# The causal mask of the score maxima: one full-array product per bank, or four products on the diagonal 32x32 parts of the array

## The chip, the cores and the metric

The kernel runs on one core of a Trainium2 chip. The metric is device time in microseconds (us) of one execution, given as the median of several runs. Engines are named as in the profile: PE is TensorE's matmul side, PEld its weight loads, DVE is VectorE, ACT is ScalarE, POOL is GpSimd, SP issues DMAs.

## The reference, cut to what matters

Sixteen sequences of 256 tokens and 128 features pass through two layers. Layer 0 has causal softmax attention with 16 heads of 8 features and a mixture of 8 experts; layer 1 has a retention block and a second mixture of experts. The change lies in layer 0's attention alone:

```python
qvk = (h @ Wqvk).reshape(b, s, 3, H, HD)
q, v, k = (qvk[:, :, 0], qvk[:, :, 1], qvk[:, :, 2])
scores = jnp.einsum('bshi,bthi->bsth', q, k)
mask = jnp.where(jnp.arange(s)[None, :] > jnp.arange(s)[:, None], -jnp.inf, 0.0)
scores = scores + mask[None, :, :, None]
weights = jax.nn.softmax(scores / math.sqrt(d), axis=2)
```

A softmax that is safe against overflow needs the largest allowed score of every row (the maximum over the keys up to the query's own position). Finding these maxima is what `top` does.

## The kernel before, in words

**Operands.** For each sequence `n`, `products` and `keys_and_queries` (L406 to L424) make `kU` and `qM`, float32 tiles of 128 partitions. Head group `j` (0 to 3) owns the 32 partitions `32*j` to `32*j+31`, so a score product of one head contracts over 32 rows: the operands are slices `[r, ...]` with `r = slice(32*j, 32*j+32)`. Such a product uses 32 of the array's 128 rows and all 128 of its columns; the profile writes it 32*128. Four products of different `j` can sit in the array beside each other. A float32 product is two instruction pairs in the trace (a weight load and a matmul each); a bfloat16 product is one pair.

**Maxima.** `top(ops, u, js, nm)` (L439) works on two head groups `js`. It takes a PSUM bank of 128 x 512 per group, first puts the causal mask into it, and then lists the score products that are added on top. The mask is made by a matmul with an identity: `ident_bf` (128x128 bfloat16) is the stationary operand, `cmask` (0 below the diagonal, -1e30 above it, four copies of 128 columns) the moving one. In `u == 0` (queries 0 to 127 against keys 0 to 127) the mask covers all 512 columns of the bank (L448); in `u` = 1 and 2 (queries 128 to 255 against all keys) it covers the second half of each of two 256-column parts (L456), 256 columns in all. `after` then reduces each bank with a DVE maximum into `nm`. Once per sequence `top_rows` transposes `nm` (tile `pm`), copies it (`mT`) and sends it by four DMAs into spare rows of `qM`, so that the weights' products subtract the maxima.

**Weights.** `weights` (L485) makes the transposed scores of the sequence before in two more banks per call, ACT takes the exponential into `pt`, and POOL zeroes what lies above the diagonal. `values` (L538) multiplies with the values (tile `av`, 128 rows by 32 columns of the array, written 128*32) and `project_out` (tile `po`) ends the attention.

**Order.** Each engine's instructions keep the order in which the Python program issues them. In the loop over `n` (L1504) six steps follow each other, three `u` by two pairs of head groups. Each step is one call of `together(top(...), weights(...))`: the two mask matmuls go out while `top` builds its list, and `together` then interleaves the products of the two lists by head group. After each step `fill()` issues a portion of other work: norms and router of layer 0, its gathered experts, the layer 1 retention of blocks that are ready. Some of that work uses the whole array (`pT`, `pxs`, `ptk`, `pret<-q,st`, `plog`), some uses 32-row parts (`psc`, `pw`). All PSUM tiles share eight banks in turn.

**After.** The masks are gone after the last sequence's maxima, at about 363 us. What follows is mostly the layer 1 experts (`ph`, `py`).

Of the kernel before, what the change touches and what calls it, by code (L numbers as in the profile page):

```python
# [21 lines left out]
P = 128  # L22
# [20 lines left out]
def two_layer_kernel(  # L43
# [26 lines left out]
    B, S, D = h.shape  # L70
# [19 lines left out]
    for t0, t1 in ((0, 2), (2, 4), (4, 8)) + tuple((t, t + 4) for t in range(8, NT, 4)):  # L90
# [7 lines left out]
    ident_bf = const.tile([P, P], BF16)  # L98
# [6 lines left out]
        out=before, in_=ones, compare_op=ALU.is_gt, fill=0.0, base=0, pattern=[[1, P]], channel_multiplier=-1  # L105
    )

    cmask = const.tile([P, 4, P], BF16)
    nc.vector.memset(cmask, 0.0)
    nc.gpsimd.affine_select(  # L110
        out=cmask, in_=cmask, compare_op=ALU.is_ge, fill=NEG, base=0, pattern=[[0, 4], [-1, P]], channel_multiplier=1
# [8 lines left out]
    for m, cmp in ((lower, ALU.is_gt), (lower_eq, ALU.is_ge)):  # L120
        nc.vector.memset(m, 1.0)
        nc.gpsimd.affine_select(
            out=m, in_=m, compare_op=cmp, fill=0.0, base=0, pattern=[[1, E], [-1, E]], channel_multiplier=0
# [36 lines left out]
    def bank(shape, name="sc"):  # L160
        return ps.tile(shape, F32, tag="sc", name=name)
# [40 lines left out]
    def matmul(*args, **kw):  # L202
        return pe.matmul(*args, **kw)
# [222 lines left out]
    def project_v(n):  # L426
# [9 lines left out]
        va4 = vas[n % 3].rearrange("p k h (d a) -> p (k h) d a", a=4)  # L436
        dve.tensor_copy(va4[:, :, :, 0:2], pv.rearrange("p k (h a d) -> p (k h) d a", a=2, d=8))

    def top(ops, u, js, nm):  # L439


        kU, qM, _ = ops
        banks = {j: bank([P, 512], "top") for j in js}
        todo = {j: [] for j in js}
        for j in js:
            r = slice(32 * j, 32 * j + 32)
            if u == 0:
                matmul(banks[j], lhsT=ident_bf, rhs=cmask.rearrange("p j k -> p (j k)"), start=True, stop=True)  # L448
                out = banks[j].rearrange("p (s a k) -> p s a k", s=2, a=2)
                for s in range(2):  # L450
                    for a in range(2):
                        todo[j].append((out[:, s, a], qM[r, s, a, 0:P], kU[r, s, 0:P], False, P))
            else:
                s = u - 1
                out = banks[j].rearrange("p (a k) -> p a k", a=2)
                matmul(out[:, :, P:S], lhsT=ident_bf, rhs=cmask[:, 0:2, :], start=True, stop=True)  # L456
                for a in range(2):
                    todo[j].append((out[:, a], qM[r, s, a, P:S], kU[r, s, :], False, S))

        def after():  # L460
            for j in js:
                if u == 0:
                    o = nm[:, 0].rearrange("p (h j) -> p h j", j=4)[:, :, j]
                    i = banks[j].rearrange("p (a k) -> p a k", k=P)
                else:
                    o = nm[:, 1].rearrange("p (h j) -> p h j", j=4)[:, 2 * u - 2 : 2 * u, j]
                    i = banks[j].rearrange("p (a k) -> p a k", a=2)
                dve.tensor_reduce(o, i, AX.X, ALU.max, negate=True)

        return todo, after  # L470
# [1020 lines left out]
    for u in range(3):  # L1491
        together(top(ops[0], u, (0, 1), maxima[0]), top(ops[0], u, (2, 3), maxima[0]))
        if u < 2:
            transpose0(u, 2 - 2 * u, 4)
# [9 lines left out]
    for n in range(B):  # L1504
# [8 lines left out]
        for u in range(3):  # L1513
            for js, others in (((0, 1), (2, 3)), ((2, 3), (0, 1))):
                parts = [weights(ops[n], u, others, pts)]
                if n + 1 < B:
                    parts.insert(0, top(ops[n + 1], u, js, maxima[n + 1]))
                together(*parts)
                next(sums, None)
                fill()  # L1520
                if n + 1 == B:
                    turn(2.0)
# [135 lines left out]
```

## Time and profile before

| | |
|---|---|
| three runs | 753.98, 760.08, 762.68 us (median 760.08) |
| profiled execution | 753.3 us, of which its span is 751.4 us |
| granted TensorE clock, mean | 0.993 |
| PE busy | 713.7 us (95%) in 5621 matmuls |
| PEld busy | 474.0 us (63%) in 5624 weight loads |
| DVE, ACT, POOL busy | 400.0, 358.6, 284.1 us |
| mask matmuls, `top<-cmask,ident_bf` | 44.4 us busy, 189 records; first at 13.6 us, last at 362.8 us |
| score products for the maxima, `top<-kU,qM` | 110.2 us busy, 1024 records |

How to read it: "busy" counts a matmul from its start to a modelled end that includes the way through the array, so busy times of matmuls in a row overlap and a busy PE is not one at its peak. The distance between the starts of two instructions says more. "x2" in a line of the timeline means that two instructions of one kind were merged; "idle before <-releaser" gives the idle time ahead of the instruction on its engine and what ended it. "issue" means that nothing in the profile explains the wait.

### The profile page before, as it was taken

To read this page: it belongs to the slowest core of one execution; us is meant where nothing else is said; L and a number is where in the kernel's file an instruction comes from. 1 tells how busy PE (TensorE), PEld (TensorE's weight loads), DVE (VectorE), ACT (ScalarE), POOL (GpSimd) and SP (SyncE) were. 2 spreads that over 40 slices of the span, in tenths; PEclk is the share of its full clock that TensorE was granted. 3 is DMA by queue.
4 is the path that set the end of the run, shared out by engine and by line. 5 is a ranking of instruction groups with operands and counts; after the bars stand their busy time and mean duration, and the time that the engine had idled before them with its cause. 6 is when DMAs were issued, how large, how long until landed. Compare 5 with 4: busy or idle time off the path is not lost.

```text
span 751.4 us, 14840 instructions
## 1 busy us (share of the span) xinstructions
PE 713.7 (95%) x5621; PEld 474.0 (63%) x5624; DVE 400.0 (53%) x1074; ACT 358.6 (48%) x707; POOL 284.1 (38%) x516
## 2 busy tenths in 40 slices
PE   5999988999999999999999989999999999999997
PEld 3556655766555566556466655666766776767675
DVE  8774876766657566676552556853223223224222
ACT  3477534555576566867665544223232222332222
POOL 3153354787556557676463413345000000121000
PEclk9999999999999999999999999999999999999999
DMA  4114464223333636404222121231000000323011
GB/s 123 23 51 132 126 174 134 36 48 41 56 62 90 147 89 155 99 14 78 60 55 54 24 60 46 69 91 34 1 28 2 1 1 1 43 32 40 31 41 43
DMA packets 79312, 45.73 MB, mean 61 GB/s; under 512 B 17112, under 2 KB 74656, under 8 KB 79232
## 3 DMA queue, kind: packets, MB, share of 16 engines
q1 hardware_dynamic: 62432, 34.84, 16.4%
q0 software_dynamic: 16800, 9.83, 9.9%
q8 instruction: 50, 0.82, 0.4%
q14 instruction: 30, 0.25, 0.1%
HBM read 24.97 MB, written 17.31 MB: 56 GB/s over the span
## 4 chain that ended last, share of the span: by engine, by line
PE 70%; DVE 13%; DMA 5%; POOL 4%; ACT 3%; issue 3%; SPq 1%; DVEq 0%; ACTq 0%; POOLq 0%
PE py L175 20%; PE ph L175 18%; PE top L175 6%; PE av L175 5%; DVE nm L175 4%; DMA x<-ytab 4%; PE wts L175 4%; PE po L175 3%; PE pq L175 2%; PE pret L175 2%; PE pk L175 2%; POOL nz L175 1%; POOL pt L175 1%; ACT xn L175 1%; SPq L175 1%
## 5 line engine op out<-in xcount | busy, mean ns | idle before, releaser
L175 ACT ACTIVATE hT<-ph,b1T 128x512 f32<-128x512 f32 (+1 forms) x134 | 90.1, 678 | 170.0 <-PE ph L175 155.5
L175 PEld LDWEIGHTS py<-fW_sb,hT 128*128 128x128 f32 x1328 | 155.3, 192 | 21.4 <-issue 19.8
L175 PE MATMUL py<-fW_sb,hT 128*128 128x128 f32 x1328 | 157.9, 276 | 0.0
L175 PE MATMUL ph<-xnT,fW_sb 128*128 128x512 f32 x320 | 147.5, 601 | 0.4 <-DVE st L175 0.4
L175 DVE TENSOR_REDUCE nm<-top 128x2 f32<-128x512 f32 (+1 forms) x192 | 122.2, 682 | 35.1 <-PE wts L175 20.5
L175 ACT ACTIVATE pt<-wts 128x512 f32<-128x512 f32 x192 | 104.9, 599 | 63.8 <-PE wts L175 45.7
L175 PE MATMUL wts<-qM,kU 32*128 32x512 f32 (+1 forms) x512 | 120.0, 526 | 1.1 <-DVE come L175 0.5
L175 POOL TENSOR_SCALAR_AFFINE_SELECT pt<-pt 128x512 f32<-128x512 f32 (+1 forms) x96 | 82.6, 882 | 96.4 <-ACT pt L175 89.4
L175 PE MATMUL top<-kU,qM 32*128 32x256 f32 (+1 forms) x1024 | 110.2, 347 | 0.5 <-issue 0.4
L175 PEld LDWEIGHTS ph<-xnT,fW_sb 128*128 128x128 f32 x320 | 58.0, 192 | 62.3 <-issue 57.3
L175 PEld LDWEIGHTS top<-kU,qM 32*128 32x128 f32 x1024 | 72.6, 187 | 30.1 <-issue 26.5
L175 DVE SCALAR_TENSOR_TENSOR x<-py,gate,x 128x128 f32<-128x128 f32 x160 | 48.6, 346 | 70.5 <-PE py L175 70.5
L175 DVE TENSOR_SCALAR hT<-ph,b1T 128x512 f32<-128x512 f32 (+1 forms) x38 | 26.6, 708 | 97.3 <-ACT hT L175 58.4
L175 POOL DMA_DIRECT2D x<-acc x8 | 10.4, 1368 | 158.0 <-issue 115.3
L175 PEld LDWEIGHTS wts<-qM,kU 32*128 32x128 f32 x512 | 47.4, 186 | 8.5 <-DVE nm L175 2.4
L175 POOL TENSOR_SCALAR_AFFINE_SELECT s<-s 128x1024 f32<-128x1024 f32 x32 | 34.9, 1112 | 36.7 <-ACT s L175 36.7
L175 PE MATMUL av<-pt,va 128*32 128x256 f32 (+1 forms) x512 | 45.4, 489 | 2.3 <-POOL pt L175 1.9
L175 PE MATMUL top<-cmask,ident_bf 128*128 128x256 bf16 (+1 forms) x189 | 44.4, 312 | 0.7 <-DVE nm L175 0.5
L175 ACT COPY s<-psc 128x512 f32<-128x512 f32 x64 | 32.7, 603 | 4.7 <-PE psc L175 4.7
L175 PEld LDWEIGHTS av<-pt,va 128*32 128x32 f32 x512 | 14.6, 109 | 28.0 <-issue 19.6
L175 ACT COPY sv<-av 128x512 f32<-128x512 f32 x32 | 18.5, 590 | 24.6 <-PE av L175 10.6
L175 PE MATMUL pq<-xnT,wqk 128*128 128x256 f32 (+1 forms) x80 | 27.4, 458 | 1.2 <-ACT xnT L175 1.1
(242 smaller groups left out, 934.6 us busy)
## 6 DMA issues: line engine op xcount, KB each, us to landing
ytab<-zeros SPq DMA_DIRECT2D x16, 256.0 KB
x<-ytab POOLq DMA_DIRECT2D x16, 256.0 KB, 4.4
fW_sb<-in_L_ffn_W_dram SPq DMA_DIRECT2D x16, 256.0 KB
xtab<-xnw SPq DMA_DIRECT2D x8, 272.0 KB
num<-sv SPq DMA_DIRECT2D x64, 32.0 KB
den<-di SPq DMA_DIRECT2D x16, 128.0 KB
xtab<-xn SPq DMA_DIRECT2D x8, 256.0 KB
acc<-zeros SPq DMA_DIRECT2D x8, 256.0 KB
```

What stands on the lines that cost most here:

```text
L175: ins = f(*args, **kw)
```

## The change

Each mask product is split into four. Part `k` takes rows and columns `32*k` to `32*k+31` of the identity as the stationary operand and the same 32 rows of `cmask` as the moving one, and writes partitions `32*k` to `32*k+31` of the bank. Since the off-diagonal blocks of an identity are zero, the four products together fill the bank as the one did. `tile_position` puts part `k` on the 32x32 part of the array at row `32*k`, column `32*k`.

```diff
+    def mask(o):
+        for k in range(4):
+            r = slice(32 * k, 32 * k + 32)
+            matmul(
+                o[r],
+                lhsT=ident_bf[r, r],
+                rhs=cmask[r, 0 : o.shape[1], :],
+                start=True,
+                stop=True,
+                tile_position=(32 * k, 32 * k),
+            )
 ...
             if u == 0:
-                matmul(banks[j], lhsT=ident_bf, rhs=cmask.rearrange("p j k -> p (j k)"), start=True, stop=True)
+                mask(banks[j].rearrange("p (k n) -> p k n", k=4))
 ...
-                matmul(out[:, :, P:S], lhsT=ident_bf, rhs=cmask[:, 0:2, :], start=True, stop=True)
+                mask(out[:, :, P:S])
```

In the built program PE's list grows from 192 to 768 mask matmuls with a weight load each. Every other instruction stands where it stood, on all engines, and the waits attached to the instructions are as many as before and of the same kinds.

## Prediction

> **What bounds the kernel now.** I read the page first (busy shares and the largest groups), then the table by stretches, PE's waits, and at last the timeline around single masks, PE and its weight loads together.
>
> ```profile
> span 751.4 us, 14840 instructions
> ...
> PE 713.7 (95%) x5621; PEld 474.0 (63%) x5624; DVE 400.0 (53%) x1074; ACT 358.6 (48%) x707; POOL 284.1 (38%) x516
> ...
> L175 PE MATMUL top<-kU,qM 32*128 32x256 f32 (+1 forms) x1024 | 110.2, 347 | 0.5 <-issue 0.4
> ...
> L175 PE MATMUL top<-cmask,ident_bf 128*128 128x256 bf16 (+1 forms) x189 | 44.4, 312 | 0.7 <-DVE nm L175 0.5
> ```
>
> PE is busy nearly all the time, and the masks wait for almost nothing (0.7 us idle in all ahead of them). From the table by stretches and PE's waits up to 366 us, where the masks lie:
>
> ```profile
> 20.00:366.00 346.00, 331.32 (x3248) 207.97 (x3243) 233.26 (x588) 215.38 (x447) 204.09 (x380) 0.99 0.37 85
> ```
>
> ```profile
> PE pT L175 <- DVE wqk L175: 8.0, 1, 8.0
> PE pm L175 <- DVE nm L175: 3.2, 5, 0.9
> PE pxs L175 <- DMA xk<-xtab,idx: 2.4, 2, 1.6
> PE av L175 <- POOL pt L175: 1.9, 2, 1.7
> ```
>
> The columns are the stretch, its length, then busy us and instructions of PE, PEld, DVE, ACT and POOL: PE works 331.3 of 346 us, DVE 233.3. Its waits for others, after the start-up one of 8.0 us, are a few us in all. So time added to PE ahead of 366 us moves the end almost one for one. Now one step of the loop in the timeline (columns: start, length, engine, operation):
>
> ```profile
> 203.19 0.39 PE L175 MATMUL top<-kU,qM 32*128 32x128 f32 x4
> ...
> 203.51 0.11 PEld L175 LDWEIGHTS <-ident_bf 128*128 128x128 bf16 x2
> 203.51 0.61 PE L175 MATMUL top<-cmask,ident_bf 128*128 128x512 bf16 x2
> ...
> 204.05 0.19 PEld L175 LDWEIGHTS top<-kU,qM 32*128 32x128 f32 x2 [0.42 <-issue]
> 204.05 0.38 PE L175 MATMUL top<-kU,qM 32*128 32x128 f32 x2
> ```
>
> The last two of the products at 203.19 start at 203.30 (a narrower window shows them). On one part of the array these follow each other every 0.11 us, so they are through at 203.41; yet the mask's weight load starts only at 203.51. The second mask starts at 203.74 (narrower window). Full 512-column masks in a row start 0.216 us apart, so it is through at 203.95, and the next load waits until 204.05. So each time the array passes from 32*128 to 128*128 or back, some 0.09 to 0.10 us are lost, and the next weights cannot be loaded ahead. I counted every such passage: from 32*128 to mask the median is 0.093 us between the end of the stream and the load's start, from mask to 32*128 it is 0.094. Now a mask after work on the full array:
>
> ```profile
> 201.35 0.71 PE L175 MATMUL po<-wo_sb,wv 128*128 128x128 f32 x4
> ...
> 201.79 0.21 PEld L175 LDWEIGHTS <-ident_bf 128*128 128x128 bf16 x2
> 201.90 0.59 PE L175 MATMUL top<-cmask,ident_bf 128*128 128x512 bf16 x2
> ```
>
> Here the identity is loaded at 201.79, under the last `po` product, and the mask follows without a gap (median 0.003 us over these passages). The kind of array part is the same, so nothing is lost. The last view is a passage that changes the columns alone, full array to 128*32:
>
> ```profile
> 216.63 0.50 PE L175 MATMUL pv<-wqvk_sb,xnT 128*128 128x128 f32 x3
> ```
>
> ```profile
> 217.06 0.16 PEld L175 LDWEIGHTS av<-pt,va 128*32 128x32 f32 x8
> 217.06 2.79 PE L175 MATMUL av<-pt,va 128*32 128x512 f32 x32
> ```
>
> **The change part by part.** The stream itself: a mask of N columns still sends N columns, now through four parts. How parts run together is shown by the two kinds that the kernel has. Products of four row parts overlap (in the step above two `top` and two `wts` start within 0.02 us), and so do four column parts writing one bank: eight `av` loads take 0.16 us, one takes 0.11, so they start 0.007 us apart. I therefore take four mask parts to start 0.007 us apart and run together, 0.216 us for 512 columns and 0.11 for 256. The second bank's part 0 follows the first bank's part 0, loaded ahead as the second four `av` weights are. The group of two masks then ends 3 x 0.007 = 0.02 us later than now. Built in order, the program has 93 such groups: 93 x 0.02 = **+1.9 us**.
>
> The passages: a group's end (mask to 32*128 products) costs 0.094 now, and I keep that. A group's start depends on what stands before it in PE's list. Of the 93, 46 follow work on parts of the array (26 `top`, 8 `psc`, 6 `pw`, 4 `pvar`, one `av`, one `pb`) and lose 0.09 already. The other 47 follow full-array work (`pT`, `po`, `pxs`, `pret<-q,st`, `ptk`, `plog` and others) and lose nothing. With 32*32 masks all 93 change the kind of part. The new loss at 47 is 0.095 us, as from `pv` to `av` above: three `pv` 0.11 apart from 216.63, the last stream over at 216.96, the `av` load at 217.06. On top, the first weights are loaded in the open: `av`'s first matmuls take 0.617 against 0.592 for later ones, 0.025 for 32 float32 columns, so about 0.013 for bfloat16, an estimate by half. 47 x (0.095 + 0.013) = **+5.1 us**. The full identity's load shows 0.011 in the open where the array was switched before, so nothing changes at the 46.
>
> The 576 further pairs need no time of their own: the trace has stretches of 64 PE instructions in 1.0 us, while the densest step (`u` = 0, 48 instructions of products and 16 of masks) will have 64 in about 1.6. No semaphore is added. The -1e30 arrives in the same bank ahead of the same products, so DVE, ACT, POOL and the queues only see PE later.
>
> Sum on PE: +7.0 us. Some of it is taken up where PE waits now: `pm` for `nm` (3.2 us in five places, after DVE reduced eight banks without a pause), `av`, `pxs`. A group adds up to 0.13 us and a sequence about 0.44, so the five `pm` waits alone could take 2.2 if DVE were not itself fed by the later products. I take 1.5, bounds 0 and 3. That leaves **+5.5 us**. The profiled execution, 753.3 us (span 751.4 and 1.9 around it), becomes 758.8. The three runs have a median of 760.1, 6.8 above the profiled one; I carry the difference over: **765.6 us**, +0.7%.
>
> What the trace does not show is a 32*32 product. Bounds: from below, a passage between 32*128 and 32*32 costs nothing since the rows are cut alike; from above, the four parts run one after another. The row nearest to the first is full array to 128*32, rows cut alike, and it loses 0.095; the rows nearest to the second are `av` (four parts, one bank) and `top` (four row parts, four banks), and both overlap. So I take neither bound for the forecast.
>
> A rule speaks against the overlap. The Trainium skill, TensorEngine Tiling (Array Packing), Restrictions and Gotchas, Gotcha 1, says that different row tiles cannot access the same PSUM bank at the same time; the four mask parts lie in different row parts and write one bank. No run here has such a case: `top` and `wts` give each row part its own bank. By that rule the sum would be the serial one of the next paragraphs, by the rows of `av` it is the one above. PSUM — Partial Sum Buffer, Terms (quadrant), in turn says that different 32-partition quadrants of one bank may be accessed at once, which is this case, and I side with that.
>
> **Rivals.** *Serial parts (slower).* If four parts that write one bank exclude each other, a 512-column mask takes 4 x 0.216 in place of 0.216, +0.65, and a 256-column one +0.32. With 64 and 128 of them that is 41 + 41 = 82 us, and with the 5.1 about 87: 847 us. For it: nothing in the trace joins row parts in one bank. Against: `av` writes four quadrants of one bank at full speed. It decides early: from 765.6 to the 1% line (767.7) only 2.1 us are missing, 0.023 us in each of 93 groups, which is a start distance of 0.015 in place of 0.007.
>
> *Free passages (faster).* If 32*32 and 32*128 need no switch, each group's end saves 0.094, and the 0.102 by which the first product's weights are loaded in the open (matmul 0.372 against 0.270): 93 x 0.196 = 18.2 us. The 41 starts after 32*128 work save 0.10 each, 4.2. Less the 7.0, PE gains 15.4: 744.7 us. DVE's reductions (2 x 0.68 = 1.36 us a step against PE's 1.39 in `u` = 1 and 2) would become the bound in part and keep up to half: 745 to 752. Against it: every passage in the trace that changes rows or columns loses 0.09 to 0.10, and only `pm` (128*16, 16 columns used of a full-array part) passes free.
>
> *Full landing.* If the waits take up nothing and the first loads cost 0.025, PE adds 7.6 us, +1.0%: 767.7, on the line.
>
> **How the numbers follow.** About 1% is what a measurement of this kernel can tell from no change: its three runs lie 1.1% apart. The forecast with its full-landing edge has 0.80, serial parts or a part of that 0.12, free passages 0.08. The forecast's own range is 757 to 773: +2 to +8 us on PE, and the median's own scatter. Of its 0.80, 0.50 lies within 1%, 0.28 above, 0.02 below. Faster 0.10, same 0.50, slower 0.40. The range of 755 to 776 leaves out the far ends of both rivals.
>
> **What would show it.** In the profile after: 768 mask matmuls, of 32*32; four starting within 0.03 us; 0.09 between the stream before and the first load at all groups, also after `po` and `pT`; two 512-column masks to the next products 0.55 us after a full-array product (0.52 now), two 256-column ones about 0.34 (0.32 now); PE's share unchanged; `pm`'s waits a little shorter. Mask parts 0.1 us or more apart would make it wrong upwards, products whose weights are loaded under the masks would make it wrong downwards.

## The result, and the profile after

The change makes the kernel slower by half a per cent. Its median is 759.68 us (756.15 to 765.59, 20 runs) against 757.26 us for the kernel before (751.12 to 762.68, 20 runs); the ratio is 1.0048 with a 95% interval of 1.0027 to 1.0069, or +3.6 us (2.0 to 5.2). Ratios and intervals, here and below, are those on record, worked out from all runs and not from the two medians (whose quotient is 1.0032 here). The profiled execution took 759.34 us, of which 757.4 are its span: 6.0 us more than the span before.

From the page of the kernel after: the span, the engines, the queue that brings instructions (columns: packets, MB, share), and the two groups of `top` on PE.

```profile
span 757.4 us, 15995 instructions
...
PE 718.9 (95%) x6200; PEld 475.9 (63%) x6200; DVE 400.5 (53%) x1074; ACT 358.4 (47%) x707; POOL 282.8 (37%) x516
...
q8 instruction: 54, 0.88, 0.5%
...
L175 PE MATMUL top<-kU,qM 32*128 32x256 f32 (+1 forms) x1024 | 109.2, 346 | 0.0
...
L175 PE MATMUL top<-cmask,ident_bf 32*32 32x256 bf16 (+1 forms) x768 | 46.4, 312 | 0.5 <-DVE nm L175 0.4
```

The masks are 768 products of 32*32, and together they are busy for 46.4 us, where 192 full ones (189 recorded) were for 44.4. So the parts run together; one after another they would have shown some 80 us more. Four packets more came through q8 (50 before), and these turn out to matter. The table by stretches and PE's waits up to 366 us, in the columns of the prediction:

```profile
20.00:366.00 346.00, 330.08 (x3740) 206.07 (x3740) 229.46 (x576) 211.20 (x437) 199.12 (x369) 0.99 0.37 85
```

```profile
PE pxs L175 <- DMA xk<-xtab,idx: 3.4, 2, 2.9
PE pm L175 <- DVE nm L175: 3.3, 6, 0.9
PE av L175 <- POOL pt L175: 2.4, 2, 2.1
```

PE's waits did not shrink: `pm` waits 3.3 us (3.2 before), and the wait of `pxs` for the first gathered tokens rose from 2.4 to 3.4. Now a mask behind full-array work in the timeline (start, length, engine, operation):

```profile
188.35 0.61 PE L175 MATMUL po<-wo_sb,wv 128*128 128x128 f32 x4
188.89 0.12 PEld L175 LDWEIGHTS <-ident_bf 32*32 32x32 bf16 x8
188.89 0.61 PE L175 MATMUL top<-cmask,ident_bf 32*32 32x512 bf16 x8
189.43 0.19 PEld L175 LDWEIGHTS top<-kU,qM 32*128 32x128 f32 x2 [0.42 <-ACT ys L175]
189.43 0.38 PE L175 MATMUL top<-kU,qM 32*128 32x128 f32 x2
```

And the next step, a mask behind products on parts:

```profile
190.20 0.39 PE L175 MATMUL top<-kU,qM 32*128 32x128 f32 x4
190.52 0.12 PEld L175 LDWEIGHTS <-ident_bf 32*32 32x32 bf16 x8
190.52 0.61 PE L175 MATMUL top<-cmask,ident_bf 32*32 32x512 bf16 x8
191.06 0.19 PEld L175 LDWEIGHTS top<-kU,qM 32*128 32x128 f32 x2 [0.42 <-issue]
```

In both cases the identity is loaded only when the array is empty (load and mask start together), and the products follow 0.54 us after the first mask. Before, the identity behind `po` was loaded under the last `po` product. Over all recorded groups, the medians from the end of the stream before to the first product after the masks are:

| what stands before the mask | mask columns | before, us | after, us | difference |
|---|---|---|---|---|
| full-array work | 256 | 0.315 | 0.423 | +0.108 |
| full-array work | 512 | 0.530 | 0.638 | +0.108 |
| work on parts | 256 | 0.417 | 0.420 | +0.003 |
| work on parts | 512 | 0.631 | 0.633 | +0.002 |

So PE's list has grown by 47 x 0.108 + 46 x 0.003 = 5.2 us. How little of it arrives is seen where the clock was full in both profiles. The trace is cut at the start of each sequence's `values` (the start of its second copy `sv<-av`):

| stretch of before, us | new passages (x 0.108) | longer after by, us |
|---|---|---|
| 45.6 to 65.0 | 3 (0.32) | -0.26 |
| 65.0 to 83.8 | 4 (0.43) | +0.64 |
| 83.8 to 104.6 | 2 (0.22) | -0.33 |
| 127.0 to 156.5 | 3 (0.32) | +0.13 |
| 156.5 to 184.0 | 5 (0.54) | +0.33 |
| 220.0 to 244.8 | 3 (0.32) | -0.08 |
| 296.6 to 368.2 | 10 (1.08) | +0.09 |
| sum | 30 (3.24) | +0.52 |

A sixth of the local cost arrives. The one stretch that stands out is 104.6 to 127.0 us, with a single new passage and +3.14 us. Something happened there that is not a passage; the experiments went after it. Not all of it need be one thing: the kernel after runs 3.41 us of this stretch at half the granted clock (from 122.5 us), the kernel before none of it.

One thing about all the numbers below: in every profile the granted clock falls to half for 3.4 us (sometimes 6.8, once 10.2) at several places that differ between profiles, and a run's mean clock explains most of the scatter between runs of one kernel (correlation -0.78; 0.01 of mean clock goes with 5.2 us). That is why each comparison needs a dozen runs, and why two spans are not compared by their difference alone.

### The profile page after: what moved, and what is told of

It reads as the page before. It is cut to its first block, busy times and chain, and to the rows that moved or that the text cites. A ratio compares the mean times of both kernels' runs of the same rounds, so it can differ in the third digit from the quotient of the medians.

```text
span 757.4 us, 15995 instructions
## 1 busy us (share of the span) xinstructions
PE 718.9 (95%) x6200; PEld 475.9 (63%) x6200; DVE 400.5 (53%) x1074; ACT 358.4 (47%) x707; POOL 282.8 (37%) x516
## 4 chain that ended last, share of the span: by engine, by line
PE 72%; DVE 11%; DMA 5%; POOL 5%; issue 2%; ACT 2%; SPq 2%; DVEq 0%; ACTq 0%; POOLq 0%
PE py L175 20%; PE ph L175 18%; PE top L175 7%; PE av L175 5%; PE wts L175 4%; DVE nm L175 4%; PE po L175 3%; PE pq L175 3%; DMA x<-ytab 2%; PE pk L175 2%; SPq L175 2%; PE pret L175 2%; DMA den<-di 1%; PE psc L175 1%; POOL nz L175 1%
## 5 line engine op out<-in xcount | busy, mean ns | idle before, releaser
L175 PEld LDWEIGHTS py<-fW_sb,hT 128*128 128x128 f32 x1328 | 157.5, 194 | 21.5 <-issue 20.1
L175 PE MATMUL py<-fW_sb,hT 128*128 128x128 f32 x1328 | 160.3, 278 | 0.0
L175 PE MATMUL ph<-xnT,fW_sb 128*128 128x512 f32 x320 | 145.8, 595 | 0.4 <-DVE st L175 0.4
L175 PE MATMUL wts<-qM,kU 32*128 32x512 f32 (+1 forms) x512 | 117.9, 525 | 0.5 <-DVE nm L175 0.3
L175 PE MATMUL top<-cmask,ident_bf 32*32 32x256 bf16 (+1 forms) x768 | 46.4, 312 | 0.5 <-DVE nm L175 0.4
```

What stands on the lines that cost most here:

```text
L175: ins = f(*args, **kw)
```

## The experiments

Where an expectation speaks of passages, it means the prediction's reason: every change of array part at a mask costs what was read from the trace. Theory C, in some of them: the kernel before had a lucky alignment that any shift spoils. Theory D: the instruction packets fall differently and one of them meets the writes ahead of the first gather.

### The change taken in halves, a probe, and the change again

The helper was made to note whether the product issued last used the full array (`kind["last"]`). The first kernel uses the four parts only behind work on parts, where no passage is added; the second only behind full-array work.

```diff
+        parts = kind["last"] == "part"      # first kernel; the second has == "full"
 ...
-                matmul(banks[j], lhsT=ident_bf, rhs=cmask.rearrange("p j k -> p (j k)"), start=True, stop=True)
+                mask(banks[j].rearrange("p (k n) -> p k n", k=4), parts)
```

> The four diagonal parts are used only for the 46 mask groups whose predecessor in PE's list is work on parts of the array; the 47 that follow full-array work keep the one full product. Theory (the change of the kind of array part ahead of a mask costs, 0.108 us each time, and only where it is new): none of the 46 is new, so within 0.3 us of before, ratio 1.000. Rival (four loads and matmuls in place of one cost by themselves, wherever they stand): 46 of 93 groups, half of the change's +3.6 us, +1.8 us, ratio 1.0024. In the trace the theory wants 0.42 us from the end of the work before to the first product at 256-column groups after part work, as before.

> The other half: diagonal parts only at the 47 groups that follow full-array work, full products at the 46 others. Theory: all of the cost of the change is here, 47 x 0.108 = 5.1 us on PE, +3.6 us in time, ratio 1.005. Rival (cost of the parts themselves): +1.8 us, ratio 1.0024.

Measured (ratio to the kernel before, in brackets its 95% interval): 1.0031 [0.9999, 1.0064] for the half without new passages (760.46 against 757.4 us) and 1.0022 [0.9991, 1.0054] for the half with all of them (759.29). The first should have been 1.000: its groups take the 0.003 us of the table, and no more, in its own trace. So there seems to be a loss that no passage makes, though the interval just reaches 1.000, and the two halves cannot be told from each other.

The third keeps full-array masks and puts one small 32x32 product ahead of each of the 47, so that the array goes to a part and back.

```diff
+        if kind["last"] == "full" and not kind.get("mask"):
+            matmul(
+                banks[js[0]][0:32, 0:64],
+                lhsT=ident_bf[0:32, 0:32],
+                rhs=cmask[0:32, 0, 0:64],
+                start=True,
+                stop=True,
+                tile_position=(0, 0),
+            )
```

> The kernel before, with one small product (32 rows, 32 columns of the array, 64 moving columns, bfloat16, overwritten by the mask at once) ahead of each of the 47 full masks that follow full-array work. Theory: two changes of kind per group, 0.095 + 0.013 + 0.027 stream + 0.09 + 0.011 = 0.236 us in place of 0.003, 47 x 0.233 = 11.0 us on PE. If a fixed share of seven tenths lands (3.6 of 5.2), +7.7 us, ratio 1.010; if waits take up a fixed 1.5 us and the rest lands, +9.5 us, 1.0125. Rival (cost by number of instructions): 47 pairs in place of the change's 576, +0.3 us, ratio 1.000.

Measured: 1.0048 [1.0018, 1.0078]. On PE each probe takes 0.233 us in the trace, 47 x 0.233 = 11 us; 3.6 us arrive. A miss, and the same lesson as the stretches above: here PE time arrives at about a third.

The change itself once more, on the chip of these three:

> The changed kernel once more beside the others, as the yardstick on this chip: +3.6 us, ratio 1.0048, between 1.0027 and 1.0069.

It gave 1.0033 [1.0002, 1.0064].

### Is it any shift at all?

The kernel before again; then the kernel before with its `po` products doubled in the first two sequences (0.9 us on PE), and in all sixteen (6.9 us).

```diff
-        for c in range(2):
-            matmul(po[:, c, :], lhsT=wv[:, c * P : c * P + P], rhs=wo_sb, start=True, stop=True)
+        for _ in range(2 if n < 2 else 1):      # the larger one: range(2)
+            for c in range(2):
+                matmul(po[:, c, :], lhsT=wv[:, c * P : c * P + P], rhs=wo_sb, start=True, stop=True)
```

> The kernel before, unchanged, as a control: ratio 1.000. If its interval leaves out 1.000, or its mean lies 2 us off, the +2 to +3 us of the first three experiments say nothing. Its profile is a second look at the stretches 127 to 156 us and 245 to 297 us, where the first look at the kernel before had other half-clock windows than the rest.

> The kernel before with the two products of the attention's output projection issued twice for the first two sequences only: four full-array product pairs more per sequence, 2 x 0.43 = 0.9 us on PE before 85 us, no new kind of part, no new wait. Theory A (time added to PE lands in part): at most +0.9 us, ratio 1.001 or less. Theory C (the kernel before is in a lucky alignment that any small shift spoils, which would explain that both halves of the change cost 2.5 us each and the whole of it no more): +2.5 us, ratio 1.003.

> The same doubling for all 16 sequences: 16 x 0.43 = 6.9 us of plain full-array products on PE, 15 of them ahead of the last mask. Theory A with the share that the change showed (clock by clock +2.9 of 5.1 us): +3 to +4 us, ratio 1.005. If all of it lands: +6.9, 1.009. Theory C: +2.5 us plus a little.

Measured: 1.0007 [0.9981, 1.0034], 1.0006 [0.9978, 1.0034] and 1.0056 [1.0033, 1.0079]. A shift of 0.9 us costs nothing that can be seen, which speaks against theory C (its 1.003 lies at the edge of the interval). Of the 6.9 us of the large one 4.2 arrive: hardly any at full clock in the stretches from 13 to 105 us, nearly all of the 0.43 per sequence after 127 us.

### The same number of instructions without a passage

Each mask as four full-array products of a quarter of the columns: 768 products, full identity, no new passage. (In its trace a group of masks takes 0.016 us longer than before, 1.4 us over the 93 groups.)

```diff
+            c = slice(k, k + 1) if n == 4 else slice(k // 2, k // 2 + 1)
+            h = slice(0, P) if n == 4 else slice(64 * (k % 2), 64 * (k % 2) + 64)
+            matmul(o[:, c, h], lhsT=ident_bf, rhs=cmask[:, c, h], start=(k == 0), stop=True, ...)
```

> Each mask as four full-array products of a quarter of its columns: as many mask matmuls and loads as the change (768), the same columns in all, no new kind of part. Theory A (the new passages cost): the loads stay hidden for 128 columns (0.053 us of stream against about 0.011 for the identity), for 64 columns (0.027) just so, within 0.5 us, ratio 1.000. Theory B (the number of instructions costs): as the change, ratio 1.003 to 1.005. Theory C: +2.5 us.

Measured: 1.0025 [1.0002, 1.0048]. Most undisturbed stretches are longer by 0.05 us or less (0.10 at most where the clock is full, but for one of 0.58), yet the stretch from 104.6 to 127 us by 3.42. What stands out without passages sits in this one place (which again holds 3.41 us of half clock). What lies there is the first gather of tokens for the experts (`xk<-xtab,idx`, POOL), which reads a table that SP's queue has just written (`xtab<-xnw`, two writes). SP and POOL in the timeline, first of before, then of after:

```profile
112.05 0.72 SPq L175 DMA_DIRECT2D xtab<-xnw  x1
112.87 0.80 SPq L175 DMA_DIRECT2D dc<-dd  x1
...
116.76 1.25 POOL L175 DMA_INDIRECT xk<-xtab,idx  x1 [3.15 <-DMA ytab<-zeros]
```

```profile
112.36 0.85 SPq L175 DMA_DIRECT2D xtab<-xnw  x1
113.31 0.98 SPq L175 DMA_DIRECT2D dc<-dd  x1
...
118.61 1.25 POOL L175 DMA_INDIRECT xk<-xtab,idx  x1 [4.29 <-DVE dr L175]
```

SP issues the last write 0.31 us later, but the gather leaves 1.85 us later: 6.25 us behind the write in place of 4.71. SP's own issues of these two DMAs take 0.13 and 0.18 us longer. The releasers named in brackets are guesses; what the gather needs is the table, and the landings in the trace settle it. The last `xtab` write lands in sixteen parts. Before, they land from 115.38 to 115.69 us, and POOL's wait for them ends at 115.72. After, fifteen land from 115.68 to 115.99, the sixteenth only at 117.53, and the wait ends at 117.56. PE then waits for the gathered rows:

```profile
119.61 0.30 PE L175 MATMUL pxs<-ident,xk 128*128 128x128 f32 x1 [0.89 <-DMA xk<-xtab,idx]
```

```profile
122.30 0.30 PE L175 MATMUL pxs<-ident,xk 128*128 128x128 f32 x1 [2.88 <-DMA xk<-xtab,idx]
```

The first line is of before, the second of after. How busy the 16 DMA engines are shows a hole at that time. The row of the DMA view for 106 to 118 us, 40 slices of 0.3 us in tenths, first of before, then of after:

```profile
DMA  0000000304001211109999999999999999999997
```

```profile
DMA  4010100020210011020899999999999629999999
```

Before, the engines are busy without a break; after, they fall to 6 and 2 tenths in two slices around 115.6 us. In the records of the instruction queue a 16 KB packet is fetched at 113.8 us in the kernel after; before, the packets near this place came at 108.7 and 123.1. More PE instructions, so the packets come at other times: that is theory D.

### Moving the packets

Pairs of a load and a product of 32 columns, put out at the very start where PE waits for its first data, move all later packets forward and take nothing from the path. They went to the kernel before (52 pairs), the half without passages (36) and the whole change (62).

```diff
         pT = bank([P, 4, P], "pT")
+        for _ in range(52 if (i, k1) == (0, 2) else 0):
+            matmul(pT[:, 3, 0:32], lhsT=ident_bf, rhs=ident_bf[:, 0:32], start=True, stop=True)
```

> The kernel before with 52 small product pairs (bfloat16, 32 moving columns, result unused) at the very start, where PE idles for 8 us: 104 more instructions on PE, no time of their own. Theory D: PE's instructions are fetched in packets of 16 KB, one for about 256 instructions, and a packet that moves while the last rows of the token table go out (110 to 117 us) holds up the first gather, PE then waits longer for it and a half-clock window follows. In the kernel before the packets start at 108.7 and 123.1 us; 104 instructions bring the second one forward to about 113.5. Theory D: the gather goes out 1.2 to 1.5 us later against the queue, +2 to +2.5 us in time, ratio 1.003. Theory without D (only array passages count): 1.000.

> The kernel with diagonal parts only after work on parts of the array (first experiment, ratio 1.0031 though its passages cost nothing new), with 36 such pairs at the start. Its packet at 111.0 us moves forward to about 107.3, the next from 128.7 to about 123. Theory D: the first gather is on time again and the loss goes, ratio 1.000 to 1.001. Without D: the loss stays, 1.003.

> The changed kernel with 62 such pairs at the start. Its packet at 113.8 us moves to about 110, the one at 130.9 to about 119, the gap just wide enough for table and gather. Theory D: of the change's loss only what the new passages cost is left, about +1 us by the stretches without half-clock windows, ratio 1.001 to 1.002. Without D: 1.0045 as before.

The half without passages lost its loss: 0.9992 [0.9958, 1.0026], with the packet at 108.5 us. The kernel before with 52 pairs gave 1.0025 [0.9998, 1.0052], but its packet came at 115.2 us, 4.2 us behind the write, and the gather was on time: it does not test the packet, but it shows what pairs can give without it. The whole change with 62 pairs had its gather on time too and still lost, 1.0031 [1.0004, 1.0057], where theory D had asked for 1.001 to 1.002 (which the interval takes in).

So the two missing tests: take the packet from the split masks, and bring it to the kernel before with 14 pairs more.

> Each mask again as four full-array products of a quarter of its columns (no new passage), and 62 pairs of a load and a product of 32 columns put out at the very start, where PE waits for its first data, so that the packet of instructions that came at 114.3 us comes about 5 us earlier. Theory D (without new passages the whole loss is the packet that meets the last writes to xtab, ahead of the first gather): the gather leaves on time against its queue, ratio 1.000 (-0.001 to +0.001). Theory N (768 mask products in place of 192 cost something of their own, wherever the packets fall): 1.0025 as without the padding.

> The kernel before with 66 dummy pairs at the start, 14 more than in the earlier attempt whose packet came at 115.2 us: the packet should come at about 113, within or just behind the last writes to xtab. Theory D: the first gather leaves 1.2 to 1.5 us late against its queue, PE waits about as much longer at pxs, and the ratio is 1.002 to 1.004, with not one mask changed. If the gather is on time and the ratio within 0.001 of 1, the packet is no cause by itself.

Split masks: 1.0009 [0.9987, 1.0031]. The kernel before with 66 pairs, its packet at 114.7 us: **1.0055 [1.0030, 1.0081]**, 760.15 against 755.67 us. Not one mask was touched. The 52 pairs with the gather on time had given 1.0025 at the same mean clock (0.986 over their runs), so some 0.3% of the 0.55% goes with the packet, as far as one such pair of kernels can tell. Its timeline and its DMA row, as above:

```profile
112.99 0.72 SPq L175 DMA_DIRECT2D xtab<-xnw  x1
113.81 1.04 SPq L175 DMA_DIRECT2D dc<-dd  x1
...
119.23 1.25 POOL L175 DMA_INDIRECT xk<-xtab,idx  x1 [4.04 <-DVE nm L175]
```

```profile
DMA  9970101000211100120208999999999996029999
```

A like hole, the same 6.24 us from write to gather. The split masks with padding, with the packet gone:

```profile
111.90 0.73 SPq L175 DMA_DIRECT2D xtab<-xnw  x1
112.74 0.79 SPq L175 DMA_DIRECT2D dc<-dd  x1
...
116.63 1.25 POOL L175 DMA_INDIRECT xk<-xtab,idx  x1 [3.60 <-DMA ytab<-zeros]
```

Ten profiles side by side (times from the traces; "after the write" counts from the start of the last `xtab` write's issue, a minus is ahead of it):

| kernel | packet, us after the write | gather, us after the write | ratio |
|---|---|---|---|
| before | -3.3 | 4.71 | |
| before again | -3.3 | 4.71 | 1.0007 |
| after | +1.5 | 6.25 | 1.0048 |
| after again | +1.0 | 6.24 | 1.0033 |
| split masks | +1.5 | 6.28 | 1.0025 |
| before, 66 pairs | +1.7 | 6.24 | 1.0055 |
| before, 52 pairs | +4.2 | 4.70 | 1.0025 |
| split masks, 62 pairs | -3.3 | 4.73 | 1.0009 |
| half without passages, 36 pairs | -3.4 | 4.71 | 0.9992 |
| whole change, 62 pairs | -3.5 | 4.73 | 1.0031 |

The gather is either 4.7 or 6.2 us behind the write, nothing between, and it is 6.2 where a packet comes 1 to 2 us behind it. In the four rows with 6.2, and in a fifth profile (the kernel without masks, below), the sixteenth part of the last table write lands 1.46 to 1.63 us behind the fifteenth; in the fifteen other profiles of this document 0.12 us behind it at most. So a late gather is one late part of the write, and the packet decides whether there is one.

The late gather is not all that lies in the stretch from 104.6 to 127 us. With the gather on time it is still longer than before by 1.87 us (split masks, 62 pairs), 2.00 (half without passages, 36) and 2.62 (whole change, 62), each with 3.41 us of half clock in it; with the gather late and 66 pairs it is longer by 2.15. The two looks at unchanged masks without half clock there, before again and 52 pairs, are 1.1 us shorter than before. The two halves without padding show the same stall at another place of SP's queue: their packets came at 111.0 and 110.7 us, and there the first `xtab` write took 1.88 us to issue (0.63 before) and a pair of `num` DMAs 2.38 us (1.12 before), so that everything behind them on the queue moved by 1.25 us.

### What the passages cost when the gather is on time

The half with all the new passages and 36 pairs, twice, and the whole change with 80 pairs:

> Diagonal parts only at the 47 groups that follow work on the full array (all of the new passages, half of the new instructions), and 36 dummy pairs at the start, so that the packet of 110.7 us comes near 106. Passages cost 47 x 0.108 = 5.1 us on PE. If the passages cost what the whole change with padding lost (+2.9 us at equal clock), the ratio is 1.003 to 1.004 although the gather is on time. If the loss of this half without padding (1.0022) was the packet alone, it falls to 1.000 to 1.001.

> The whole change with 80 dummy pairs at the start in place of 62, so that the packets come near 107 and 119 us. Taken apart and with the packet moved, the two halves gave 0.9992 (parts after work on parts) and 1.0012 (parts after full-array work). If the two halves add up once the packet is away from the writes and the gather, the ratio is 1.000 to 1.001, and the 1.0031 of the padding with 62 came from where its packets fell. If the whole change costs more than its halves whatever the packets do, it is 1.003 again.

> The padded half with all 47 new passages once more, beside the run above on one chip, since the two are to be compared with each other: 1.0012 before. If the 46 other groups cost nothing once the packet is away, the two kernels of this call agree within 0.0015.

All three had the gather 4.71 to 4.74 us behind the write. They gave 1.0012 [0.9989, 1.0036], 1.0028 [0.9999, 1.0057] and 1.0023 [0.9997, 1.0048]; the last two, on one chip, agree within 0.0005, so the 46 other groups cost nothing that can be seen. With the 1.0031 of the whole change and 62 pairs, four runs with all 47 passages and a gather on time have a mean of 1.0024: some 1.8 us of the 5.1 that the passages put on PE.

What the packet adds to that shows in the mean times less those of the kernel before, taken to the same mean clock by the 5.2 us for 0.01 (each good to 0.8 to 1.4 us; for the first comparison the clocks of the kernel before are not on record):

| | gather on time, us | gather late, us |
|---|---|---|
| no new passage | -0.5 (before again), -0.3 (52 pairs), +0.1 (half, 36 pairs), +0.7 (split masks, 62 pairs) | +2.5 (split masks), +2.3 (66 pairs) |
| all 47 passages | +3.0 (change, 62 pairs), +1.4 (half, 36 pairs), +2.4 (change, 80 pairs), +2.0 (half again) | +2.3 (change again) |

Either one alone costs some 2.3 us, and both together no more than one. In the change itself, moving the packet saved nothing that can be told from the scatter: 1.0031 and 1.0028 with the gather on time, 1.0048 and 1.0033 without. So the passages are enough to explain most of the loss, a late gather would be too, and the two do not add. That both end in the same wait at `pxs` would explain it, but was not tested apart.

### In the other direction: fewer masks, fewer passages

No masks at all (the maxima are taken over all keys):

```diff
-                matmul(banks[j], lhsT=ident_bf, rhs=cmask.rearrange("p j k -> p (j k)"), start=True, stop=True)
 ...
-                        todo[j].append((out[:, s, a], qM[r, s, a, 0:P], kU[r, s, 0:P], False, P))
+                        todo[j].append((out[:, s, a], qM[r, s, a, 0:P], kU[r, s, 0:P], s + a == 0, P))
```

> The kernel before without any mask in the maxima: they are taken over all 128 or 256 keys of a block in place of the allowed ones. A common shift cancels in the softmax, so the result is the reference's as long as no masked score stands far above the allowed ones. On PE the 93 groups save 0.22 to 0.63 us each by the medians of the kernel before, 35 us, and 0.1 of open weight load at the 46 that follow work on parts, 5 us: 40 us. If the maxima's reductions on DVE (8.2 us a sequence) do not bind, -40 us, ratio 0.947; if half of it meets waits, -20 us, 0.974. For the theory of the array passages it is the bound on what any form of mask can cost.

Measured: 0.9990 [0.9956, 1.0024]. By the medians above the 93 groups take some 40 us of PE's list, passages included, and leaving all of it out gains nothing that can be measured. Where it went is in the rows of its page and cores (the granted clock in tenths over 40 slices, then span and mean clock):

```profile
PEclk9899997999999999999999999999999999999999
```

```profile
core 0: 749.6 us, clock 0.979
```

```profile
L175 PE MATMUL top<-kU,qM 32*128 32x256 f32 (+1 forms) x1024 | 123.8, 357 | 1.5 <-DVE nm L175 0.8
```

The granted clock dropped: 0.9732 on average over its twelve runs, against 0.9885 over all runs of the kernel before. At 5.2 us for 0.01 that is 8 us given back; the products for the maxima, the same 1024, are busy for 123.8 us in place of 110.2. The rest of the 40 us went to waits in many places, which were not followed further. Its gather met a packet too (1.55 us behind the write, 6.11 us to the gather).

The last one keeps the full masks and puts those of all four banks out together, 48 groups of four for 93 of two, as a version that might beat both.

```diff
+            ahead4 = masked(u, (0, 1, 2, 3)) if n + 1 < B else None
 ...
-                    parts.insert(0, top(ops[n + 1], u, js, maxima[n + 1]))
+                    parts.insert(0, top(ops[n + 1], u, js, maxima[n + 1], ahead4))
```

> From the kernel before, full-array masks, but the masks of all four banks of a step pair are put out together ahead of the first pair's products: 48 groups of four in place of 93 of two, so about 45 fewer passages into and out of the full array. By the passage prices read from the trace each pair of passages that goes saves PE 0.09 + 0.09 and the first product's open load 0.10, some 0.28 x 45 = 12.6 us; by what other savings and losses on PE have kept in these runs (a third to a half), 4 to 6 us: ratio 0.992 to 0.995. If four banks held from the start make PE wait for DVE's maxima, the saving turns into waits for nm: 1.00 to 1.01.

Measured: 1.0167 [1.0135, 1.0199], 769.14 us: a clear loss, beyond even the pessimistic end. From its groups:

```profile
L175 DVE TENSOR_REDUCE nm<-top 128x2 f32<-128x512 f32 (+1 forms) x192 | 122.1, 682 | 53.7 <-PE wts L175 36.0 <-PE top L175 17.5
...
L175 PE MATMUL top<-cmask,ident_bf 128*128 128x256 bf16 (+1 forms) x191 | 41.3, 316 | 5.2 <-DVE nm L175 2.1 <-DVE slot L175 1.1 <-ACT pt L175 0.8
```

PE's waits ahead of the masks rose from 0.7 to 5.2 us, and DVE sat idle ahead of its maxima for 53.7 us in place of 35.1. That fits the expectation that four of the eight banks, held from the start of a step, make PE wait for DVE; it was not tested apart. No version found here beats the kernel before.

## Why the prediction was right and wrong

Time: 765.6 us forecast, 759.68 measured, inside the range of 755 to 776. Of the 5.9 us between them 2.8 come from the median of three runs that it started from (760.08; with 20 runs 757.26), 1.9 from the sum (+5.5 against +3.6), and the rest from a ratio that is not that of the two medians.

- **The call was wrong.** I gave no change the largest chance (0.50, slower 0.40), and the change is a loss of 0.48%. The failed step is the size of what a measurement can tell: I took 1% from the spread of three runs; twenty against twenty resolve 0.2%. My own sum of +5.5 us pointed to slower.
- **Four parts run together: right.** Four parts of one bank start within 0.010 us (188.89: eight masks in 0.61 us, as two before), and the serial rival of 847 us is out. So, for this case, is the reading of Gotcha 1 (the Trainium skill, TensorEngine Tiling (Array Packing), Restrictions and Gotchas) by which the serial sum was made: these row tiles write four different quadrants of one bank at full speed. That agrees with PSUM — Partial Sum Buffer, Terms (quadrant), that different quadrants of one bank may be accessed at the same time; but that row speaks of two engines, not of parts of the array, so to side with it was partly luck.
- **Every start of a group behind full-array work pays 0.108 us: right**, in the medians of both widths. Free passages (744.7 us) are refuted: 32*32 to 32*128 loses 0.09.
- **The stagger, +1.9 us: wrong.** Parts start 0.003 us apart, not 0.007, and the way out of 32*32 takes 0.089, not 0.094. What is left at a group behind work on parts is 0.003 us where I had 0.02: 0.1 us over 46 groups.
- **What waits take up, 1.5 us: too small.** Of the passages' 5.1 us some 3 did not arrive, as much as my upper bound for the whole 7.0. "Time added to PE ahead of 366 us moves the end almost one for one" was read off a busy share of 331 in 346 us. Added PE time arrived at 0.5 of 3.2 us (stretches at full clock), about 1.8 of 5.1 (whole runs, gather on time), 3.6 of 11 (probe), 4.2 of 6.9 (`po` doubled). And the takers I named, the `pm` waits, did not shrink: 3.2 to 3.3 us.
- **"The 576 further pairs need no time of their own": wrong**, and not where I looked. PE did issue them fast enough. But they bring four more instruction packets and move all others, and one of them came just behind the writes that the first gather needs: the gather left 1.5 us late. "The queues only see PE later" left that out. Bringing such a packet to the kernel before, with no mask changed, gave 1.0055, where pairs with the gather on time gave 1.0025.

That the sum's +5.5 us lies within 2 us of the measured +3.6 is partly luck: too much PE time was counted as arriving, and a second cost that hardly adds to the first was not seen.

## What to carry to other kernels

A busy share of 95% does not mean that time added to the engine arrives: before pricing an edit at one for one, double some harmless work of known size on that engine and see what share of it lands. An edit that changes the number of instructions also moves the fetches of instructions; if a loss sits in one stretch with none of the edited code in it, look there for a hole in the DMA row and compare the distance from a write to its reader in both traces. And settle how fine the measurement is from many runs before calling a half per cent "no change".

## What was not expected of the hardware

- Instructions come in packets of 16 KB on a DMA queue of their own (0.82 MB in 50 packets before, 0.88 in 54 after). A packet 1 to 1.7 us behind a write of the table made the gather that reads it leave 6.24 to 6.28 us behind the write in place of 4.7, in each of the four profiles of the table where it happened: fifteen of the sixteen parts of the write landed as usual, one some 1.6 us later. At other moments SP needed some 1.25 us longer to issue a DMA. Why one part is late, and why the other transfers pause meanwhile (the two slices of the DMA row), is not shown by these traces.
- Four 32*32 parts that write one bank start 0.003 us apart at full speed, while each change of the kind of part costs 0.09 to 0.10 us, also between 32*32 and 32*128.
- Less work did not mean less time: without the masks the granted clock averaged 0.9732 in place of 0.9885. In the profile after, a stretch of half clock followed the late gather at once, but the half without passages with 36 pairs has one in the same place with the gather on time, and the kernel before has none (columns as in the table by stretches; the granted clock is the 0.57, 0.58 and 1.00):

```profile
122.00:126.00 4.00, 3.22 (x9) 2.52 (x10) 1.01 (x2) 1.07 (x3) 3.50 (x5) 0.57 0.20 44
```

```profile
122.00:126.00 4.00, 4.00 (x18) 3.01 (x20) 0.50 (x2) 2.33 (x4) 3.52 (x5) 0.58 0.21 50
```

```profile
122.00:126.00 4.00, 4.00 (x38) 2.50 (x40) 1.17 (x3) 2.32 (x5) 3.52 (x5) 1.00 0.18 46
```

What goes with it is PE's wait for the first gathered rows. In five of the twenty profiles PE waits there for 0.34 to 0.89 us, and no half clock follows. In the fifteen others it waits for 1.17 to 3.25 us, and a half-clock stretch begins between 120.8 and 123.8 us in all but the kernel without masks, where one had begun at 113.2. That the wait brings the half clock is suggested by this, not shown: no run was made to tell, and every kernel has such stretches elsewhere.
